# A gather-bound recommender kernel: the far weights moved behind the ids on one queue, and the last steps of TensorE put in another order with a second PSUM bank

## The chip, the cores and the metric

The kernel runs on one core of a Trainium2 chip. The metric is the device time of that core in microseconds, the median of repeated executions. All executions of this study were in the state called fast. They still fall into two kinds: on two occasions the kernel before took 13,197 to 13,298 us (medians), on three others 11,252 to 11,276 us, and within one occasion its runs were alike to 1.1%. Four of the five occasions are on record with a chip number, and the four chips differ; no chip was met twice, so whether the kind belongs to the chip or to the occasion is not shown. The two kinds are called **stall chips** and **quiet chips** below, and no total of one kind is compared with one of the other except to say how they differ.

## The reference

For each of 16,384 rows there are 69 ids of a user's history and one label id. Cut to what matters:

```python
u   = emb[batch_user]                      # (B, 69, 96)
ql  = emb[batch_label[:, 0]]               # (B, 96)
z   = concat([q, u, q - u, q * u])         # q is ql, repeated for the 69 fields
h   = dice(z @ W1 + b1, a1)                # 384 -> 64
att = (h @ W2 + b2) @ W3 + b3              # one number per field
pre = where(batch_user < ITEM_NUM, u * att, 0)
pooled = einsum('gf,bfe->bge', window, pre)           # 69 fields into 10 groups
h = dice(bn(concat([pooled, ql]) @ Wf1 + bf1), af1)   # 1056 -> 200
h = dice(bn(h @ Wf2 + bf2), af2)                      # 200 -> 80
return h @ Wf3 + bf3
# dice(x, a) = (a * (1 - p) + p) * x   with p = sigmoid(x), up to a constant near 1
```

## The kernel before

The rows are fetched by GpSimd (POOL), 128 at a time, with indirect DMAs: 8,832 gathers for the history and 128 for the labels. TensorE transposes each gathered tile, computes the hidden layer for a pair of chunks (8 gathers), turns it into attention rows, spreads these over partitions, and sums ("pools") the rows by group with the gathered tile as weights. There are 1,104 pairs in 32 blocks of 512 rows; after each block the top layers run.

The start. The ids of the first block and the near weights (those of the attention part) go on the queue of SyncE, the far weights (those of the top layers) on that of ScalarE. Nine small constants of the top layers' dice are made from the far weights on VectorE (DVE), in program order ahead of the first label columns:

```python
ids = {0: const.tile([P, NCOL], I32, name="ids0")}
nc.sync.dma_start(out=ids[0], in_=idx0)            # 140 KB
...
nc.sync.dma_start(out=wn, in_=near)                # 236 KB
wf = const.tile([P, FAR.width], F32, name="wf")
nc.scalar.dma_start(out=wf, in_=far)               # 1,209 KB
...
dice1 = [dice_weights(b, a, f"dice1_{i}") for i, (b, a) in enumerate(zip(bf1c, af1c))]
dice2 = dice_weights(bf2c, af2c, "dice2")
...
qs[0] = head_gather(0)         # 4 gathers of label rows
head_turn(0, qs.pop(0))        # 4 transposes, then DVE copies them to qT
head_rows(0)
```

The end. The last block's top layers run in four quarters of 128 rows, each in two halves (h = 0, 1) of 16 matrix products, written by the trace as 32 matmul records. A half is followed by its dice: two activations on ScalarE (ACT), then one DVE operation that reads the half's PSUM bank. All halves share the pool `ps_m`, which has one bank:

```python
ps_h = ctx.enter_context(tc.tile_pool(name="ps_h", bufs=2, space=PSUM))
ps_m = ctx.enter_context(tc.tile_pool(name="ps_m", bufs=1, space=PSUM))
...
def top1(n, cols, h, part, p1):
    if part == 0:
        p1 = ps_m.tile([DH, BLK], F32, tag="m", name=f"p1_{n}_{h}_{cols.start}")[:, cols]
    for k in range(part * KTOP // 4, (part + 1) * KTOP // 4):
        ...
        nc.tensor.matmul(p1, w[:, h * DH : (h + 1) * DH], x, start=(k == 0), stop=(k == KTOP - 1))
    if part < 3:
        return p1
    dice(x1s[n][:, h, cols], g1, p1, bf1c[h], dice1[h])
...
# quarter[r] is a list of steps: 0..3 first half, 4..7 second half, 8 layer 2, 9 layer 3
d = NPAIR
at(d, pool_of(c + 4), hidden_of(c + 7), pool_of(c + 5), *quarter[2][0:4], rows_of(c + 6, 2), *quarter[2][4:8])
at(d, quarter[2][8], spread_of(c + 6, 2), quarter[2][9], quarter[3][0])
at(d, pool_of(c + 6), pool_of(c + 7), lambda: store(B // P - 1), *quarter[3][1:])
```

In the trace TensorE's matmuls follow this order, and `quarter[2][4]` starts only after DVE has read the bank of `quarter[2][3]` (at 13139.47 us, after 0.39 us of waiting).

## Time and profile before

| Kernel before | |
|---|---|
| three runs | 13260.15, 13297.63, 13308.35 us |
| profiled execution | 13170.6 us |
| PE busy / POOL busy | 66% / 64% |
| from the rows of quarter 2 (L353) to the end | 13138.03 to 13170.6: 32.6 us |

The prediction shows the lines of the page and of both timelines. Two views that it does not show are worth having. The first is the list of what POOL waited for in this profile (columns: line, releaser, then total us, number of waits, longest wait in us):

```profile
POOL u L257 <- issue: 2367.4, 7751, 1.5
POOL u L257 <- remote: 978.9, 318, 7.4
POOL u L257 <- PE acc L397: 462.2, 107, 39.8
POOL u L257 <- PE ptr L313: 434.0, 201, 5.7
```

The first line is the 0.3 us between two gathers, thousands of times. The second, the largest of the rest, is of waits whose releaser the profile could not name. The last two are waits for TensorE: POOL had to stop until TensorE freed a buffer, once for 39.8 us. The second view is the busy time in the stretch from 20 to 160 us, in the columns named in the prediction:

```profile
20.00:160.00 140.00, 23.73 (x68) 8.52 (x68) 11.61 (x21) 10.74 (x16) 100.12 (x107) 0.59 0.18 38
```

TensorE has 68 matmul records in 140 us, while POOL makes 107 gathers at its usual pace and fills its buffers. TensorE stands still. For most of these stops the trace says only "issue", but for one it names a releaser, a copy on ScalarE that frees a PSUM bank:

```profile
168.25 1.09 PE L313 MATMUL ptr<-ident,u 128*96 128x128 f32 x4 [26.09 <-ACT uT L325]
```

So TensorE does not stand alone: ScalarE and DVE stand too. The first sigmoid of the hidden layer (L344) starts at 68.90 us, 31.1 us after the end (37.81) of the last matmul record that it needs, and ScalarE was idle for the last 19.8 of them. Over all 1,104 pairs ScalarE sat idle for 3.1 us on average between that end and the sigmoid; in f_after, a run on a quiet chip below, it is 0.05 us. By the trace, whose matmul ends are modelled, the stall lies between TensorE's results and the engines that read them.

### The profile page before, as it was taken

How to read it: one execution, taken by the hardware profiler on the slowest of the kernel's cores; microseconds unless marked ns; L12 is line 12 of the kernel's file. 1: busy time of each engine (PE TensorE's matmuls, PEld its weight loads, DVE VectorE, ACT ScalarE, POOL GpSimd, SP SyncE). 2: the span in 40 equal slices, each digit the busy share in tenths (PEclk: the TensorE clock that was granted, in tenths of full speed). 3: DMA queues.
4: the chain of work that ended last, by engine and by line, in shares of the span. 5: the costliest groups of instructions: out<-in, count | busy, mean ns of one | idle time of the engine just before them, and what ended most of it. 6: DMA issues, size and time to landing. Idle time of an engine off the chain costs nothing.

```text
span 13170.6 us, 108463 instructions
## 1 busy us (share of the span) xinstructions
PE 8747.3 (66%) x41797; PEld 4554.2 (35%) x41797; DVE 3029.0 (23%) x5325; ACT 3167.1 (24%) x4969; POOL 8455.0 (64%) x8966
## 2 busy tenths in 40 slices
PE   3666666667666676666766667666666666676667
PEld 2333333333333333333333333333333333333334
DVE  2222222222222222222222222222222222222222
ACT  1222222222222222222222222222222222222222
POOL 6666666666666666666666666666666666666664
PEclk6777777777777777767777777777777777777777
DMA  1111111111111111111111111111111111111111
GB/s 40 35 35 34 34 34 37 34 36 34 34 36 34 35 35 35 37 34 34 35 34 37 33 35 34 34 36 35 35 35 33 36 34 35 35 35 35 35 34 22
DMA packets 288946, 454.19 MB, mean 34 GB/s; under 512 B 143538, under 2 KB 143922, under 8 KB 288306
## 3 DMA queue, kind: packets, MB, share of 16 engines
q0 software_dynamic: 286720, 440.98, 16.0%
q8 instruction: 335, 5.49, 0.2%
q1 hardware_dynamic: 1570, 5.04, 0.1%
q14 instruction: 177, 1.45, 0.0%
q10 hardware_dynamic: 144, 1.24, 0.0%
HBM read 446.61 MB, written 0.07 MB: 34 GB/s over the span
## 4 chain that ended last, share of the span: by engine, by line
PE 54%; issue 20%; another core or an unknown queue 16%; POOL 4%; ACT 3%; DVE 3%; DMA 1%; DVEq 0%; POOLq 0%
PE acc L397 11%; PE ptr L313 9%; PE ph L338 9%; PE ph L342 8%; PE p L436 7%; PE prow L353 4%; POOL u L257 3%; PE patt L370 1%; DVE quT L316 1%; PE pa L362 1%; ACT uT L325 1%; ACT y L345 1%; PE ph L335 1%; PE pc L290 1%
## 5 line engine op out<-in xcount | busy, mean ns | idle before, releaser
L257 POOL DMA_INDIRECT u<-in_rows,ids x8832 | 8333.2, 944 | 4552.4 <-issue 2367.4
L397 PE MATMUL acc<-rw,u 128*96 128x20 f32 x16384 | 1922.1, 260 | 1844.3 <-issue 1436.2
L397 PEld LDWEIGHTS acc<-rw,u 128*96 128x96 f32 x16384 | 1911.1, 197 | 2083.9 <-issue 1613.1
L313 PE MATMUL ptr<-ident,u 128*96 128x128 f32 x8832 | 1594.5, 316 | 1395.4 <-issue 1099.1
L325 ACT COPY uT<-ptr 96x512 f32<-96x512 f32 x2208 | 1283.3, 581 | 3091.3 <-DVE quT L316 1905.9
L313 PEld LDWEIGHTS ptr<-ident,u 128*96 128x96 f32 x8832 | 1079.1, 143 | 2732.2 <-issue 2182.7
L344 ACT ACTIVATE y<-ph 128x512 f32<-128x512 f32 x1104 | 659.3, 597 | 5104.0 <-remote 2661.7
L342 PE MATMUL ph<-quT,wn 96*64 96x512 f32 x4416 | 1693.6, 744 | 165.9 <-issue 158.6
L346 DVE TENSOR_TENSOR y<-ph,y 128x512 f32<-128x512 f32 x1104 | 763.5, 692 | 4287.1 <-ACT y L345 2399.0
L338 PE MATMUL ph<-uT,A 128*64 128x512 f32 x4096 | 1631.8, 800 | 145.8 <-issue 142.8
L316 DVE TENSOR_TENSOR quT<-ptr,qT 96x512 f32<-96x512 f32 x2048 | 1337.6, 680 | 1419.3 <-remote 892.2
L406 DVE COPY pooled<-acc 96x160 f32<-96x160 f32 x1008 | 429.6, 426 | 3547.6 <-remote 2121.3
L345 ACT ACTIVATE y<-y,wn,na1c 128x512 f32<-128x512 f32 x1104 | 897.8, 813 | 36.7
L342 PEld LDWEIGHTS ph<-quT,wn 96*64 96x64 f32 x4416 | 449.0, 172 | 1201.8 <-issue 1199.3
L353 PE MATMUL prow<-y,v 128*32 128x512 f32 x2208 | 629.5, 787 | 254.1 <-issue 150.2
L436 PE MATMUL p<-pooled,wf 96*100 96x512 f32 (+1 forms) x1400 | 616.5, 583 | 0.0
L338 PEld LDWEIGHTS ph<-uT,A 128*64 128x64 f32 x4096 | 280.6, 162 | 683.7 <-issue 664.9
L355 ACT COPY row<-prow 128x512 f32<-128x512 f32 (+1 forms) x277 | 161.8, 584 | 1421.8 <-remote 878.8
L370 PE MATMUL patt<-ident,row 128*128 128x128 f32 x1108 | 241.2, 338 | 277.6 <-issue 203.7
L436 PE MATMUL p<-pre,V 96*100 96x512 f32 (+1 forms) x700 | 372.7, 665 | 40.6 <-issue 25.8
L436 PEld LDWEIGHTS p<-pooled,wf 96*100 96x100 f32 x1400 | 233.7, 179 | 291.7 <-issue 291.6
L375 DVE SCALAR_TENSOR_TENSOR rw<-patt,bb,wn 128x320 f32<-128x320 f32 x554 | 273.4, 534 | 142.2 <-remote 64.3
(66 smaller groups left out, 2139.8 us busy)
## 6 DMA issues: line engine op xcount, KB each, us to landing
u<-in_rows,ids POOLq DMA_INDIRECT x8832
ids<-in_idx SPq DMA_DIRECT2D x8, 560.0 KB
q<-in_emb,ids POOLq DMA_INDIRECT x128
wf<-in_far ACTq DMA_DIRECT2D x1, 1209.0 KB
wn<-in_near SPq DMA_DIRECT2D x1, 236.0 KB
ids<-in_idx SPq DMA_DIRECT2D x1, 140.0 KB
out<-r SPq DMA_DIRECT2D x1, 63.5 KB
out<-r SPq DMA_DIRECT2D x1, 0.5 KB
```

The costliest lines, as they stand in the source:

```text
L257: nc.gpsimd.indirect_dma_start(out=dst, out_offset=None, in_=table, in_offset=bass.IndirectOffsetOnAxis(ap=index, axis=0),)
L313: nc.tensor.transpose(ptr[:, t * P : (t + 1) * P], u[:, 4 * j + t, :], ident)
L316: nc.vector.tensor_tensor(quT[:, j, :].rearrange("e (s f) -> e s f", f=FM), ptr.rearrange("e (s f) -> e s f", f=FM), by_field(q[:, k * NS ...
L325: nc.scalar.copy(uT[j][0:E], ptr)
L338: nc.tensor.matmul(p, As[n % 2][:, k // 4, :], uT[j], start=True, stop=False)
L342: nc.tensor.matmul(p, Wp, quT[:, j, :], start=False, stop=True)
L344: nc.scalar.activation(y, ph, AF.Sigmoid, scale=S_DICE)
L345: nc.scalar.activation(y, y, AF.Identity, bias=a1c, scale=na1c)
L346: nc.vector.tensor_mul(y, ph, y)
L353: nc.tensor.matmul(pr[32 * k : 32 * (k + 1), :], v2, ys[b + k], start=True, stop=True)
L397: nc.tensor.matmul(pa[:, j, 2 * t : 2 * t + 2, :].rearrange("e n g -> e (n g)"), u[:, 4 * j + t, :], rw[:, t, j, :], start=True, stop=True,)
L436: nc.tensor.matmul(p1, w[:, h * DH : (h + 1) * DH], x, start=(k == 0), stop=(k == KTOP - 1))
```

## The change

The intent at the start is to let the first gather go sooner: ids first, then near weights, then the 1,209 KB that nobody wants yet, all on one queue. The intent at the end is to fill TensorE's waits for dice with independent work (the attention rows' spread and the last two pools), and to let a second half start while the first half's bank is still being read. The instructions are the same in kind and number; they only move.

```diff
-    nc.scalar.dma_start(out=wf, in_=far)
+    nc.sync.dma_start(out=wf, in_=far)
...
         if part == 0:
-            p1 = ps_m.tile([DH, BLK], F32, tag="m", name=f"p1_{n}_{h}_{cols.start}")[:, cols]
+            banks, tag = (ps_h, "h") if n == NBLK - 1 and cols.start >= BLK // 2 and h == 1 else (ps_m, "m")
+            p1 = banks.tile([DH, BLK], F32, tag=tag, name=f"p1_{n}_{h}_{cols.start}")[:, cols]
...
-    at(d, pool_of(c + 4), hidden_of(c + 7), pool_of(c + 5), *quarter[2][0:4], rows_of(c + 6, 2), *quarter[2][4:8])
-    at(d, quarter[2][8], spread_of(c + 6, 2), quarter[2][9], quarter[3][0])
-    at(d, pool_of(c + 6), pool_of(c + 7), lambda: store(B // P - 1), *quarter[3][1:])
+    at(d, pool_of(c + 4), hidden_of(c + 7), pool_of(c + 5), *quarter[2][0:4], rows_of(c + 6, 2), quarter[2][4])
+    at(d, spread_of(c + 6, 2), *quarter[2][5:8], pool_of(c + 6), quarter[2][8], pool_of(c + 7))
+    at(d, quarter[2][9], quarter[3][0], lambda: store(B // P - 1), *quarter[3][1:])
```

## The prediction

> **What bounds the kernel now.** I read the page first (busy shares, slices, costliest groups), then the busy time by stretch, then the timelines of the first 70 us and the last 40 us, then the chain of work that ended last, in order of time, over the same last 40 us.
>
> The page says that no engine is full:
>
> ```profile
> PE 8747.3 (66%) x41797; PEld 4554.2 (35%) x41797; DVE 3029.0 (23%) x5325; ACT 3167.1 (24%) x4969; POOL 8455.0 (64%) x8966
> L257 POOL DMA_INDIRECT u<-in_rows,ids x8832 | 8333.2, 944 | 4552.4 <-issue 2367.4
> ```
>
> A gather costs 0.94 us on POOL and 0.30 us until the next, 1.25 us in all; 8960 gathers (8832 rows, 128 labels) at 1.25 us are 11,200 us, well under the span of 13,170.6 us. So POOL waits some 1,970 us for buffers that TensorE frees. TensorE sets the pace: 1,104 pairs of chunks in 13,170 us are 11.9 us a pair against 10.0 us of gathers, and its clock is at 0.73 on average, with stalls that the trace calls only "issue" (at the start, two pairs take 44.8 us, for example from 81.45 to 126.25 us). The change touches none of this steady part. It touches the first 10 us and the last 38 us, so this is a prediction of about ten microseconds in 13,300.
>
> The start, from the timeline of the first 70 us:
>
> ```profile
> 0.74 0.40 ACTq L155 DMA_DIRECT2D wf<-in_far  x1
> 0.75 0.40 SPq L142 DMA_DIRECT2D ids<-in_idx  x1
> 1.21 0.44 SPq L153 DMA_DIRECT2D wn<-in_near  x1
> ...
> 7.04 1.10 POOL L257 DMA_INDIRECT q<-in_emb,ids  x1 [5.73 <-DMA ids<-in_idx]
> 7.26 0.22 DVE L163 TENSOR_TENSOR Cq<-wn 96x64 f32<-96x64 f32 x1 [5.18 <-DMA wn<-in_near]
> ```
>
> POOL can gather nothing before the first ids (140 KB) are there, and waits 5.73 us for them; the 1,209 KB of far weights, wanted by nobody then, go beside them from the other queue. The trace's DMA packet records, read by queue, show it: far weights from 2.0 to 6.4 us, ids from 3.0 to 6.5 us with some engines' last one at 6.42 us, near weights from 5.9 to 7.1 us.
>
> The end, from the timeline of the last 40 us. Columns: start, duration, engine, line; in brackets the idle time just before and what ended it.
>
> ```profile
> 13135.75 2.35 PE L436 MATMUL p<-pooled,wf 96*100 96x128 f32 x20
> 13138.03 1.05 PE L353 MATMUL prow<-y,v 128*32 128x512 f32 x4
> ...
> 13139.47 1.34 PE L436 MATMUL p<-pre,V 96*100 96x128 f32 x10 [0.39 <-DVE x L421]
> ...
> 13144.58 0.67 PE L447 MATMUL p<-x,wf 100*80 100x128 f32 x4 [1.37 <-DVE x L421]
> ...
> 13146.60 0.38 PE L455 MATMUL p<-wf,x 80*128 80x1 f32 x2 [0.97 <-DVE x L421]
> ...
> 13147.32 1.46 PE L436 MATMUL p<-pre,V 96*100 96x128 f32 x8 [0.33 <-DVE res L456]
> 13148.57 2.64 PE L397 MATMUL acc<-rw,u 128*96 128x20 f32 x16
> 13151.73 2.75 PE L397 MATMUL acc<-rw,u 128*96 128x20 f32 x16 [0.52 <-DVE pooled L406]
> ...
> 13160.54 1.33 PE L436 MATMUL p<-pre,V 96*100 96x128 f32 x10 [1.37 <-DVE x L421]
> ```
>
> All gathers are done by then (the last is issued at 13051.5 us), and TensorE's own order is the path: every wait shown is one for the dice step of a top half or for an eviction, and the two pools that could fill them stand behind them in the order. The busy time by stretch (columns PE, PEld, DVE, ACT, POOL, then clock) adds the second cost:
>
> ```profile
> 13139.50:13144.60 5.10, 3.73 (x33) 3.52 (x33) 0.35 (x1) 1.09 (x3) 0.00 (x0) 1.00 0.00 0
> 13144.60:13148.60 4.00, 2.70 (x19) 2.32 (x20) 1.06 (x4) 0.85 (x2) 0.00 (x0) 0.92 0.00 0
> 13148.60:13154.50 5.90, 5.38 (x34) 5.27 (x34) 0.42 (x1) 0.00 (x0) 0.00 (x0) 0.50 0.01 3
> 13154.50:13160.50 6.00, 4.67 (x25) 4.46 (x25) 1.03 (x3) 0.86 (x2) 0.00 (x0) 0.69 0.04 11
> ```
>
> After the gappy stretch around 13144 us the clock is halved: sixteen pool matmuls take 2.45 to 2.75 us there and 1.46 us at full clock (13128.05 us).
>
> **What the Trainium skill says.** "DMA: Bandwidth & Descriptors", section "Queues, rings and completion order": each DMA engine goes round the queues that have work, packet by packet, and takes one queue's descriptors in order. The packet records above agree: two queues interleaved from 3.0 us on; on one queue the ids should pass first. "TensorE: Matmul & The Clock Gate", section "Part 1: The HAM clock gate": an idle window of about 3.4 us sends the array to half clock. The stretch at 0.50 agrees in kind, though TensorE was busy for 2.70 of the 4.00 us before it. "Perfetto Trace Analysis", section "Optimizing Tensor Performance": independent matmul groups should rotate through different PSUM banks so that an eviction overlaps the next group. That is what the second halves' own bank does; before, the first matmul of a second half waits for the DVE that reads the first half (13139.47 and 13160.54 us).
>
> **The change, part by part.**
>
> Start. Far weights now go behind ids and near weights. The first packet of the queue that was served first came 2.01 - 0.74 = 1.3 us after its issue, so ids packets could start at 2.0 us (at 3.0 us if that queue is simply slower). They are 128 packets of 55 ns over 16 engines, 8 x 55 ns = 0.45 us, so the last ends at 2.5 to 3.4 us instead of 6.46. From there to the gather took 7.04 - 6.46 = 0.6 us. First gather at 3.1 to 4.0 us: **3.0 to 3.9 us earlier**. Near weights follow in 8 x 78 ns = 0.6 us, so the set-up on DVE moves as much. Far weights: 8 packets an engine at 429 ns are 3.4 us, done near 7.5 us; their first reader in DVE's order is the nine dice constants (10.45 us before), ahead of the copy of qT (14.03 us before, about 10.6 us after). No wait expected. I count 3 us, as the stalls of the first 170 us may swallow a little.
>
> End. I walk TensorE's new order at full clock from the end of the first half of quarter 2, at 13138.1 us = 0. A top matmul costs 3.75 us / 32 = 0.117 us. Rows (1.0) to 1.0; first 8 matmuls of the second half, in the other bank without a wait (0.94), to 1.9; spread (0.46) to 2.4 (its row copy is ready at 1.64); 24 more (2.8) to 5.2; pool (1.46) to 6.65 in place of the dice wait of 1.3; layer 2 (0.66) to 7.3; pool (1.46) to 8.8 in place of the next dice wait (eviction of the former pool ends at 7.1); layer 3 (0.3) to 9.1; a wait until 9.45 for DVE, which now evicts the pool (0.42) before it reads layer 3 (0.20); 8 matmuls to 10.4; the store's transpose (0.3) to 10.7; 24 to 13.5; second half of quarter 3, no wait, 3.75 to 17.25. From there to the end nothing changes: 13170.6 - 13164.3 = 6.3. Sum 23.6 us, against 13170.6 - 13138.1 = 32.5 before. **End 8.9 us shorter.** Of these, about 5 us are waits (0.4 + 1.4 + 1.0 + 0.5 + 1.4, and the DVE wait of 0.3 stays) and 4 us are the half clock (1.0 + 1.3 of the pools, 0.5 of the eight, some 1.3 of the 24). As no TensorE wait above 0.5 us is left before the last dice, the half clock should not come; if it does, 5 us remain. I take 8.
>
> Sum: 3 + 8 = 11 us, 13297.6 - 11 = **13287 us**. No instruction is added or removed; work only moves.
>
> **The rivals.** (1) The ids gain does not reach the end: TensorE paces the kernel and stalls for 20 us at a time in the first 170 us, POOL fills all its buffers by about 152 us and then waits. For it: POOL is ahead anyway. Against: TensorE's own first transposes wait for gathers of that moment (1.0 to 1.2 us idle each, "DMA u"), so its whole start moves. Then 8 us are left: 13290 us. (2) The half clock stays in the tail, as its windows may fall otherwise: end 4 to 5 us shorter, 13290 to 13292 us. (3) Far weights or something behind them become a wait at the start: they land beyond 11 us and hold DVE in front of qT; loses 1 to 2 us of the 3. (4) Noise rules: the three runs before span 48 us, and the profiled execution took 13172 us, 1% less. TensorE's stalls, not the work, make that spread, and a shift of 3 us at the start can deal them anew. This is the largest term by far for the time that will be read.
>
> **Range and chances.** The mechanism gives 13285 to 13293 us; the spread of runs gives about 25 us either way for a median of three, with a longer tail downwards because of the profiled execution. Range 13225 to 13330 us. A step of 2% is 266 us, more than twice the gap between the fastest execution seen and the median: 0.02 faster, 0.97 within 2%, 0.01 slower.
>
> **What would show it right or wrong.** In the changed profile: first gather at 3 to 4 us, not 7.04, with the idle time before it near 2 us; near weights' first reader at about 4 us; nine dice constants without an idle time ahead of them. In the tail: no DVE x wait before the first matmul of a second half; two pools at about 1.5 us each; clock 1.00 from the last pool to the last second half; about 24 us from the end of quarter 2's first half to the end of the span. It would be wrong if ids still land after 5 us, if a second half waits for its bank, if the clock is again 0.50 after the pools, or if the whole time moves by more than 100 us, which the changed parts cannot explain.

## The result, and the profile after

| Same chip, six runs each | before | after |
|---|---|---|
| median, us | 13289.36 | 13282.84 |
| range, us | 13260.15 to 13308.35 | 13243.29 to 13305.56 |
| ratio after/before | | 0.9994, 95% interval 0.9975 to 1.0012 |

Ratios are the mean time of one kernel's fast runs over that of the other's of the same rounds, so not quite the ratio of the medians quoted. The verdict is "same"; the interval is about 24 us either way and cannot show a gain of 11. The two profiled spans (13170.6 before, 13284.2 after) must not be subtracted: they differ by 114 us because of stalls far from the changed parts. What can be compared is the changed parts themselves.

The start, from the timeline of the profile after (columns as in the prediction):

```profile
1.68 0.42 SPq L155 DMA_DIRECT2D wf<-in_far  x1
...
3.23 1.10 POOL L257 DMA_INDIRECT q<-in_emb,ids  x1 [1.92 <-DMA ids<-in_idx]
3.92 0.22 DVE L163 TENSOR_TENSOR Cq<-wn 96x64 f32<-96x64 f32 x1 [1.85 <-DMA wn<-in_near]
...
9.53 0.15 DVE L222 TENSOR_SCALAR dice<-wf 100x1 f32<-100x1 f32 x1 [2.35 <-DMA wf<-in_far]
...
9.85 0.42 PE L281 MATMUL pq<-ident,q 128*96 128x128 f32 x1 [3.26 <-DMA q<-in_emb,ids]
...
12.70 0.69 DVE L282 COPY qT<-pq 96x512 f32<-96x512 f32 x1 [2.53 <-PE pq L281]
```

The first gather is at 3.23 us instead of 7.04, and the near weights' first reader at 3.92 instead of 7.26. But DVE now waits 2.35 us for the far weights, and the copy to qT is at 12.70 us, only 1.3 us before the 14.03 of the kernel before. The trace's DMA packet records, on the zero of the timeline, suggest why. On the one queue the ids pass first, from 1.77 to 2.61 us; the far weights' packets run from 3.06 to 8.94 us, and the first packet of a gathered label row comes at 7.38 us, 4.2 us after the gather started. Before, that was 9.06 - 7.04 = 2.0 us, and the far weights were out of the way by 6.17 us. So the label rows seem to wait in the DMA engines beside the far weights; `f_held` below tests it.

The end, from the timeline of TensorE in the profile after (the two added lines make L436 into L438, L447 into L449):

```profile
13259.66 1.05 PE L353 MATMUL prow<-y,v 128*32 128x512 f32 x4
13260.64 1.12 PE L438 MATMUL p<-pre,V 96*100 96x128 f32 x8
...
13264.78 1.46 PE L397 MATMUL acc<-rw,u 128*96 128x20 f32 x16
13266.08 0.68 PE L449 MATMUL p<-x,wf 100*80 100x128 f32 x4
13266.76 1.53 PE L397 MATMUL acc<-rw,u 128*96 128x20 f32 x16
...
13268.84 1.14 PE L438 MATMUL p<-pre,V 96*100 96x128 f32 x8 [0.34 <-DVE res L458]
...
13270.85 3.51 PE L438 MATMUL p<-pooled,wf 96*100 96x128 f32 x20
13274.20 1.25 PE L438 MATMUL p<-pre,V 96*100 96x128 f32 x10
```

Neither second half (13260.64 and 13274.20) has an idle time ahead of it. The two pools take 1.46 and 1.53 us instead of 2.64 and 2.75, with layer 2 between them. The one wait left in this stretch is 0.34 us. From the rows (L353) to the end of the span it is 13284.2 - 13259.66 = 24.5 us, against 32.6: 8.1 us shorter. The twenty matmuls at 13270.85 take 3.51 us, though, where the same group takes 2.35 at full clock. The busy time by stretch, same profile:

```profile
13261.10:13266.20 5.10, 5.10 (x52) 4.89 (x51) 0.97 (x3) 1.12 (x3) 0.00 (x0) 1.00 0.00 0
13266.20:13270.20 4.00, 3.66 (x33) 3.31 (x33) 1.29 (x5) 0.86 (x2) 0.00 (x0) 0.95 0.01 4
13270.20:13274.20 4.00, 4.00 (x26) 4.00 (x25) 0.29 (x1) 0.00 (x0) 0.00 (x0) 0.62 0.05 14
13274.20:13277.90 3.70, 3.70 (x36) 3.64 (x34) 0.35 (x1) 0.87 (x3) 0.00 (x0) 1.00 0.01 2
```

TensorE was busy in 3.66 of the 4.00 us from 13266.2, and still its mean clock in the next 4 us was 0.62. In the trace's clock records the granted clock is only ever 1.00 or 0.50, in pieces of 3.41 us or multiples of it (but for the last piece): before, it is 0.50 from 13147.94 us for 10.24 us, after, from 13269.81 us for 3.41 us. The lowered clock has shrunk, not gone.

So the local intervals moved as intended: 3.8 us at the first gather, 8.1 us in the tail. What is open is whether both arrive in the total, and which part of the change does what.

### The profile page after: what moved, and what is told of

Same layout as the page of the kernel before. It is cut to its first block, busy times and chain, and to the rows that moved or that the text cites. A ratio compares the mean times of both kernels' runs of the same rounds, so it can differ in the third digit from the quotient of the medians.

```text
span 13284.2 us, 108461 instructions
## 1 busy us (share of the span) xinstructions
PE 8859.7 (67%) x41797; PEld 4576.5 (34%) x41797; DVE 3037.9 (23%) x5325; ACT 3167.4 (24%) x4969; POOL 8476.9 (64%) x8966
## 4 chain that ended last, share of the span: by engine, by line
PE 54%; issue 21%; another core or an unknown queue 14%; POOL 5%; DVE 3%; ACT 2%; DMA 1%; DVEq 0%; POOLq 0%
PE acc L397 11%; PE ptr L313 9%; PE ph L338 9%; PE ph L342 9%; PE p L438 7%; POOL u L257 5%; PE prow L353 4%; PE patt L370 1%; DVE quT L316 1%; PE pa L362 1%; ACT uT L325 1%; PE ph L335 1%; PE pc L290 1%; ACT y L345 1%
## 5 line engine op out<-in xcount | busy, mean ns | idle before, releaser
L313 PE MATMUL ptr<-ident,u 128*96 128x128 f32 x8832 | 1637.3, 319 | 1651.3 <-issue 1300.8
L342 PE MATMUL ph<-quT,wn 96*64 96x512 f32 x4416 | 1722.9, 749 | 211.3 <-issue 200.3
L353 PE MATMUL prow<-y,v 128*32 128x512 f32 x2208 | 669.4, 785 | 285.0 <-issue 187.8
L438 PE MATMUL p<-pooled,wf 96*100 96x512 f32 (+1 forms) x1400 | 621.5, 587 | 2.4 <-issue 2.4
L438 PE MATMUL p<-pre,V 96*100 96x512 f32 (+1 forms) x700 | 368.8, 664 | 23.1 <-issue 13.1
L438 PEld LDWEIGHTS p<-pooled,wf 96*100 96x100 f32 x1400 | 236.4, 181 | 295.0 <-issue 294.8
```

What stands on the lines that cost most here:

```text
L313: nc.tensor.transpose(ptr[:, t * P : (t + 1) * P], u[:, 4 * j + t, :], ident)
L342: nc.tensor.matmul(p, Wp, quT[:, j, :], start=False, stop=True)
L353: nc.tensor.matmul(pr[32 * k : 32 * (k + 1), :], v2, ys[b + k], start=True, stop=True)
```

## The experiments

Theory: both gains reach the end and add up. Rival: TensorE paces the kernel, so an earlier first gather is swallowed, and only the end counts. A further rival is that the far weights, now in the way of the label rows, cost what the ids gained.

### A short version, to get the noise out (s_before, s_after, s_start, s_end)

Each is cut to two blocks (69 pairs, 1,024 rows). They are **wrong on purpose**: the other rows of the output are never written, so the relative error is nan. `s_start` has the far weights' queue alone, `s_end` the new order and the second bank alone.

```diff
-NPAIR = NBLK * NCH // 2
+NRUN = 2
+NPAIR = NRUN * NCH // 2
+FIRST = (NPAIR - 8) % 4      # lines up the groups of four pairs at the end
...
-        if n == NBLK - 1 and k >= EARLY:
+        if n == NRUN - 1 and k >= EARLY:
```

> The kernel before, cut to its first two blocks of rows (69 pairs of chunks instead of 1,104; the other 15,360 results are not written, so it is wrong on purpose), so that its start and its end are the same instructions but the steady part, whose stalls make the spread of 50 us, is one sixteenth as long. All theories: about 69 pairs at 11.9 us and some 80 us of slow first pairs, an estimate of 850 to 950 us, with a spread of runs of a few us instead of 50. Start and tail as in the full kernel: first gather near 7.0 us, copy of qT near 14.0 us, 32 to 33 us from the end of quarter 2's first half to the end of the span.

> The changed kernel cut in the same way. Theory A (both parts reach the end): 9 to 11 us less than the cut kernel before, about 1%: some 8 us from the tail, 1 to 3 us from the start. Theory B (only the tail reaches the end, the start is swallowed by TensorE's stalls in the first 170 us): 7 to 9 us less. Theory C (the stalls are dealt anew by any shift, and the changes are lost in it): less than 4 us apart, or an order of the runs that does not repeat.

> Cut kernel with the start part of the change alone (far weights on the ids' queue, behind ids and near weights). The profile of the full changed kernel has the first gather at 3.23 us, 3.8 us earlier, but the copy of qT only 1.3 us earlier (12.70 against 14.03 us). Theory S1 (gathers set the start): 3 to 4 us less than the cut kernel before. Theory S2 (the first gathers' rows wait behind the far weights on the DMA engines): about 1.3 us less in the start, and 0 to 2 us less in all. Theory S3 (the stalls swallow it): 0 us, within 1 us.

> Cut kernel with the end part of the change alone (new order and the second halves' own bank). Theory A and B: 7 to 9 us less than the cut kernel before, the tail 24 to 25 us long instead of 32 to 33, and within 2 us of the whole change. Rival (half clock stays in the tail): tail 27 to 29 us, 4 to 5 us less in all.

| four runs each | median, us | minus s_before | last gather starts | rows of quarter 2 to the end |
|---|---|---|---|---|
| s_before | 771.20 | | 707.1 | 32.3 |
| s_start | 764.10 | -7.1 | 703.5 | 32.4 |
| s_end | 763.33 | -7.9 | 707.7 | 24.4 |
| s_after | 752.98 | -18.2 | 703.3 | 25.8 |

The absolute time missed my expectation: 771 us, because this chip had no long stalls. The kernel before at full size took 11252.48 us on it (7 runs). The signs are clear, the sizes are not: s_before alone spreads from 762.39 to 772.70 us, and by means instead of medians the differences are -5.3, -6.7 and -16.0. What the profiles add is more exact: the start part moves the last gather by 3.6 us and leaves the tail alone, the end part does the opposite. The list of POOL's waits in s_before explains why the start reaches the end here:

```profile
POOL u L259 <- issue: 159.4, 523, 0.3
```

The gaps between gathers are of 0.3 us; the only longer wait of POOL is the 5.2 us for the first ids. On this chip the gathers are the bound, not TensorE.

### The parts at full size on a quiet chip (f_after, f_start, f_end, f_order)

All give correct results. `f_after` is the change itself; the others are the kernel before with one part: `f_start` the queue line, `f_end` the order and the bank, `f_order` the order alone, with all halves left in `ps_m`.

```diff
 f_start:
-    nc.scalar.dma_start(out=wf, in_=far)
+    nc.sync.dma_start(out=wf, in_=far)
 f_order:
-    at(d, pool_of(c + 4), ..., *quarter[2][4:8])      # the three old lines
+    at(d, pool_of(c + 4), ..., quarter[2][4])         # the three new ones
 f_end: the lines of f_order, and
+            banks, tag = (ps_h, "h") if n == NBLK - 1 and cols.start >= BLK // 2 and h == 1 else (ps_m, "m")
```

> The whole change at full size, again, in case it meets a chip without TensorE's long stalls, such as the one of the cut kernels, where the kernel before took 11,252 us and repeated to about 5 us. There POOL never waits for a buffer, so gathers at 1.25 us set the pace and both ends of the kernel add in full. Theory Q (gathers bound on such a chip): 3.8 us from the start and 7 to 8.5 us from the tail, 11 to 12.5 us less than before (0.10 to 0.11%). Theory R (the cut kernels' 18 us hold at full size): 15 to 20 us less. On a chip with the stalls: within 0.3% of before, sign unclear.

> Start part alone at full size. Gathers bound: 3.5 to 4 us less than before, equal to the earlier first gather (7.04 to 3.23 us), although the first label rows reach TensorE only 1.3 to 2.4 us earlier. Rows behind the far weights bind instead: about 1.3 us less. On a chip with the stalls: unclear.

> End part alone at full size. Gathers bound: the last gather is issued at the same time as before, and the tail from the end of quarter 2's first half to the end is 24 to 25.5 us instead of 32.3: 7 to 8.5 us less. On a chip with the stalls the tail is the same in the profile, the total unclear.

> New order of the end alone, at full size, without the bank of its own: first and second halves share one bank as before. By the walk through TensorE's order both halves' dice waits of 1.4 us come back (in quarter 2 rows fill 1.0 us of it, so 0.4 us), the rest of the gain stays: tail 25 to 27 us, 5.5 to 7 us less than before. Rival (the bank is what matters and the order alone only moves waits): less than 3 us.

The chip was quiet: the kernel before 11254.23 us (65 runs, 11250.55 to 11260.55).

| | median, us (runs) | minus before | ratio, 95% interval | rows of quarter 2 to the end |
|---|---|---|---|---|
| f_after | 11240.27 (21) | -14.0 | 0.9987, 0.9980 to 0.9994 | 24.3 |
| f_start | 11250.12 (13) | -4.1 | 0.9995, 0.9987 to 1.0004 | 32.6 |
| f_end | 11244.77 (21) | -9.5 | 0.9990, 0.9984 to 0.9997 | 24.6 |
| f_order | 11247.95 (21) | -6.3 | 0.9993, 0.9986 to 0.9999 | 27.1 |

**The parts add up**: 4.1 + 9.5 = 13.6 against 14.0 (by means 5.0 + 10.2 = 15.2 against 14.7). f_after falls between its two theories, and f_end's 9.5 us is above the 7 to 8.5 expected. The interval of f_start alone still includes no change, so the profile is asked as well. All gathers of f_start, then of f_end (columns: count, shortest/median/longest in ns, start of the first and of the last in us):

```profile
L257 POOL DMA_INDIRECT u<-in_rows,ids x8832: 940/944/1096, 8.4 to 11189.3; - x197
```

```profile
L257 POOL DMA_INDIRECT u<-in_rows,ids x8832: 940/944/1092, 12.4 to 11192.5; - x197
```

With the far weights behind the ids the first row gather is 4.0 us earlier and the 8,832nd still 3.2 us earlier. So most of it arrives. f_after agrees with its last gather at 11189.0, f_order (without the queue line) with 11192.7. These 3.2 us and the 8.0 us of f_end's tail make 11.2, less than the 14.0 of the totals. The profiles show where such a difference can come from: the stretch from the last gather to the rows of quarter 2, which no edit touches, took 21.3 us in f_after, 27.9 in f_start, 31.4 in f_end and 31.5 in f_order, at mean clocks of 1.00, 0.87, 0.84 and 0.84. Single profiles of different kernels can therefore not be subtracted here either; the medians of 13 to 65 runs average this out in part. In f_after POOL's waits begin with

```profile
POOL u L257 <- issue: 2532.8, 8311, 0.3
...
```

and all others too, but for the 1.9 us for the first ids, have a longest of 0.3 us. Compare a steady millisecond of f_after, and then of the kernel before on the stall chip (POOL's busy column is the fifth, `755.89 (x802)`; the 0.76 and 0.74 behind it are TensorE's clock):

```profile
5000.00:6000.00 1000.00, 802.46 (x3764) 410.81 (x3762) 274.42 (x469) 285.31 (x445) 755.89 (x802) 0.76 0.20 41
```

```profile
5000.00:6000.00 1000.00, 698.84 (x3250) 357.85 (x3251) 234.65 (x408) 243.94 (x383) 649.89 (x690) 0.74 0.17 35
```

802 gathers in 1,000 us are 1.247 us each, which is what a gather and its gap take (0.944 + 0.30): POOL never stops. On the stall chip there are 690, and TensorE does less in the same time at nearly the same mean clock. The stretch from 20 to 160 us of f_after stands against the 68 matmul records of the kernel before on the stall chip:

```profile
20.00:160.00 140.00, 96.58 (x359) 42.23 (x359) 50.26 (x100) 37.07 (x57) 106.04 (x112) 0.63 0.20 40
```

There are 359, at a clock of 0.63 against 0.59: the stall is not a slow clock.

The tail part of the change is about the same on both kinds of chip. The start part is in full view only where gathers are the bound.

In f_order the two waits that the shared bank causes are there still:

```profile
11225.67 1.12 PE L436 MATMUL p<-pre,V 96*100 96x128 f32 x8 [0.39 <-DVE x L421]
...
11240.95 1.34 PE L436 MATMUL p<-pre,V 96*100 96x128 f32 x10 [1.37 <-DVE x L421]
```

Their sum, 1.76 us, is most of the 2.5 us between the tails of f_order (27.1) and f_end (24.6). By total time the bank on top of the order is worth 11247.95 - 11244.77 = 3.2 us (by means 2.3, each mean with a standard error of 0.8 to 0.9).

How much harm do the far weights do by the time it matters? The first matmuls of the hidden layer, in f_after and then in f_end:

```profile
31.03 1.98 PE L338 MATMUL ph<-uT,A 128*64 128x512 f32 x4
```

```profile
34.48 1.98 PE L338 MATMUL ph<-uT,A 128*64 128x512 f32 x4
```

The lead is 3.45 us, though the copy to qT started only 2.3 us earlier (11.85 against 14.19). The matmul needs the eight gathers of its pair, and these follow POOL's clock, not that of qT.

### The bank alone, and two repairs of the start (f_bank, f_held, f_small)

`f_bank` is the kernel before with the second bank and the old order. `f_held` is the change with the far weights issued only after the first pair, and their readers moved back. `f_small` is the change with the first ids split, so that the 2 KB of label ids travel ahead of the rest.

```diff
 f_bank (to the kernel before):
+            banks, tag = (ps_h, "h") if n == NBLK - 1 and cols.start >= BLK // 2 and h == 1 else (ps_m, "m")
 f_held (to the change):
-    nc.sync.dma_start(out=wf, in_=far)
...
+    def far_load():
+        nc.vector.memset(wf[0:1, 0:1], 0.0)
+        nc.sync.dma_start(out=wf, in_=far)
...
+    at(1, far_load)
+    at(3, far_prep)                 # the nine dice constants
-        at(2 + 2 * f, lambda f=f: tail_weights(f))
+        at(4 + 2 * f, lambda f=f: tail_weights(f))
 f_small (to the change):
-    nc.sync.dma_start(out=ids[0], in_=idx0)
+    lab0 = const.tile([P, NQ], I32, name="lab0")
+    nc.sync.dma_start(out=lab0, in_=idx0[:, NT:NCOL])
+    nc.sync.dma_start(out=ids[0][:, 0:NT], in_=idx0[:, 0:NT])
...                                 # the first label gathers read lab0
```

> The bank of its own for the second halves alone, in the old order, at full size. By the walk it removes the 0.4 us wait in quarter 2 and the 1.4 us wait in quarter 3: tail (from quarter 2's rows to the end) 30.8 us instead of 32.6, 1.8 us less in all; the half clock of the pools stays, since the dice waits before layers 2 and 3 stay. Rival (bank and order are independent, each worth what it adds to the other): 3.2 us less, the difference between the medians of the whole end part and of the order alone.

> The whole change, but the far weights are loaded only after DVE's work on the first pair (a one-element write to their tile by DVE holds the transfer back), and their readers come later. In the changed kernel the first label rows waited behind the far weights on the DMA engines: first gather 3.25 us, its rows at TensorE 9.1 to 9.9 us. Held back, rows should land some 2.3 us after their gather as before the change, TensorE's first transpose of labels near 6 us and the copy of qT near 10.5 us instead of 12.3. Theory G (the pace of gathers is the path, TensorE catches up with it within the first pair): the total is within 2 us of the whole change. Rival (the rows that waited are on the path): 1.5 to 2.5 us less than the whole change.

> The whole change, with the first ids split: the four label columns in a transfer of their own (2 KB), the rest behind it. If the path at the start is issue, landing, first gather: the first gather starts at 2.5 to 2.8 us instead of 3.25, all gathers follow, 0.5 to 0.7 us less than the whole change, too small to be sure of in the total but plain in the profile. Rival (the 280 columns cost nothing, it is the landing that takes the time, or the fifth gather now waits for the second transfer): first gather unchanged, or idle time before the first row gather.

This chip had the stalls: the kernel before 13197.48 us (51 runs, 13163.47 to 13255.01).

| | median, us (runs) | ratio, 95% interval | rows of quarter 2 to the end |
|---|---|---|---|
| f_bank | 13199.03 (22) | 0.9998, 0.9989 to 1.0006 | 30.3 |
| f_held | 13197.11 (14) | 0.9993, 0.9980 to 1.0005 | 24.3 |
| f_small | 13188.95 (22) | 0.9991, 0.9983 to 0.9999 | 24.2 |

No total here decides anything about ten microseconds: the standard deviation of one run is 19 us, against 2.7 us on the quiet chip. f_small, which contains the whole change, is 11 us below the kernel before by means (13188.2 against 13199.3), of the size of the quiet chip's gain, at the edge of its interval. f_held contains it as well and is 5.7 us below by means. The local intervals decide more.

*f_bank.* The tail shortens by 2.3 us, from 32.6 to 30.3, between the 1.8 of the walk and the 3.2 of the rival. The pools stay where they were, and slow:

```profile
13147.96 2.64 PE L397 MATMUL acc<-rw,u 128*96 128x20 f32 x16
13151.11 2.75 PE L397 MATMUL acc<-rw,u 128*96 128x20 f32 x16 [0.51 <-DVE pooled L406]
```

These are the durations of the kernel before, and of f_start, which has the old order on a quiet chip. So the lowered clock at the pools does not come from the waits at the bank. At the pools it goes when the order changes (1.46 and 1.48 us in f_order, where the bank's waits remain); further on, f_order still has one piece of 3.41 us at half clock, from 11234.41 us.

*f_held.* The far weights' packets ran from 32.87 to 36.83 us, out of the way. The first label packet came at 5.04 us, 1.8 us after the first gather at 3.24, and the copy to qT started at

```profile
10.64 0.69 DVE L288 COPY qT<-pq 96x512 f32<-96x512 f32 x1 [3.51 <-PE pq L287]
```

That is 2.1 us earlier than in the profile after, and it is the 10.6 us that the prediction had worked out without the far weights' traffic. **The traffic is the cause** of the later head (the label rows' way to qT). The edit holds back the far weights and, behind them on the queue, the next blocks' ids (two loads of 560 KB). The far weights are the likelier part: in the profile before, packets of the next ids ran from 6.23 to 9.57 us, and the label rows still came after 2.0 us. The first hidden matmul was at 31.08 us. In the profile after it comes only at 70.39, behind a stall, so the run to compare with is f_after (31.03, on a quiet chip): the gain seems gone within the first pair.

*f_small.* The first gather was at 2.92 us instead of 3.23; I had expected 0.5 to 0.7 us from it and got 0.3. The bytes of the ids are a small part of what the first gather waits for.

### Both repairs on a quiet chip (f_both)

`f_both` is the change with f_held's and f_small's edits together. It tells whether the pace of the gathers is all there is (then only f_small's few tenths of a microsecond come on top of the change), or whether an earlier head is worth its 2 us as well.

> The whole change with both additions to its start: far weights held back, and the label columns of the first ids in a transfer of their own. First gather near 2.9 us as in the run with the split ids, the labels' rows some 2.3 us after their gathers as in the run with the far weights held back, copy of qT near 10.3 us. On a chip without the long stalls (before 11,250 to 11,260 us): theory G (pace of gathers is the path) 14 to 15 us less than before, as the whole change with 0.3 us more; rival (late label rows are on the path) 16 to 17 us less. On a chip with the stalls (before near 13,200 or 13,290 us): 5 to 20 us less, which tells nothing between the two.

The chip was quiet: the kernel before 11276.48 us (25 runs), f_both 11261.18 us (21 runs), ratio 0.9987, 0.9980 to 0.9994. That is 15.3 us by medians and 14.8 by means, against 14.0 and 14.7 for the change on another quiet chip. From its timeline:

```profile
2.75 1.10 POOL L265 DMA_INDIRECT q<-in_emb,lab  x1 [1.44 <-DMA lab<-in_idx]
...
9.79 0.69 DVE L290 COPY qT<-pq 96x512 f32<-96x512 f32 x1 [2.21 <-PE pq L289]
```

The head is 2 us earlier than in f_after (11.85 us) and the first gather 0.5 us, but the first hidden matmul (30.14 us) only 0.9 us earlier than in f_after and 0.3 us than in f_start, and the total follows the gather. The margin to the rival is about 1 us across two chips, so this is support rather than proof. As a version to use, f_both has no gain over the change that these runs can show.

## Why the prediction was right, and where it was not

**The size and the verdict.** 13287 us was predicted, 13282.84 measured, within 2% as expected. On its own that proves little, since the runs' spread hides the change, and that the two are so close is partly luck: the 13297.6 from which the 11 us were taken became 13289.4 with three more runs. The quiet chip gives it: 14.0 us against the 11 counted, of which the start 4.1 against 3 and the end 9.5 against 8. Both sizes had been cut back for doubts. The uncut ones (3.0 to 3.9, and 8.9) are nearer.

**First gather at 3.1 to 4.0 us.** Right: 3.23 us, with small errors that nearly cancel. All packet times of the prediction are 0.25 us late against the timeline (far weights from 1.76 to 6.17 us, ids from 2.72 to 6.22, near weights from 5.63 to 6.82). So from issue to first packet it was 1.0 us and not 1.3, while in the profile after the ids' packets took 0.84 us (1.77 to 2.61) and not 0.45; from the last packet to the gather it was 0.6 us, as counted.

**"TensorE sets the pace."** True of the profile it was read from, where POOL waits in stretches of up to 39.8 us. Not true of the kernel: on three quiet chips the gathers are the bound and no wait of POOL after that for the first ids exceeds 0.3 us in the profiles read. The 44.8 us from 81.45 to 126.25 are one pair (8 transposes and 8 hidden matmul records), not two. Rival 1, that the ids' gain does not reach the end, is refuted there by the last gather (3.2 us earlier in f_start than in f_end). On stall chips it stays undecided, as rival 4, noise, said it might.

**Far weights done near 7.5 us, no wait.** The reader was at 9.53 us after a wait of 2.35, so this failed in the profile after; in f_after the same reader was at 7.70 us after 0.58. The step that failed was the transfer's rate: eight packets an engine at 429 ns, back to back, as if the engines were theirs alone. The packet records of the profile after show the next ids' packets among them from 6.48 us and the label rows' from 7.38; how much of the delay is due to these, and why f_after was spared, is not separated. It also overlooked the opposite effect, that the label rows come later: 4.2 us from gather to first packet instead of 2.0. So rival 3 happened, and cost the head 1 to 2 us as it said (qT at 12.70 us in the profile after and 11.85 in f_after, instead of 10.6). It did not cost the total, because the head is not the path: f_end and f_after still differ by 3.45 us at the first hidden matmul.

**The tail.** Predicted 23.6 us from the end of the first half of quarter 2, measured 24.5 (the first half ends at 13259.73). The order of TensorE's steps, the fillers and the DVE wait of 0.3 us (0.34) were as walked. The term that was off is the clock: the twenty matmuls took 3.51 us instead of 2.35, and 1.16 us is a little more than the whole gap of 0.9. "As no TensorE wait above 0.5 us is left before the last dice, the half clock should not come" was wrong; the clock sank to 0.62 after a stretch that was 92% busy (3.66 of 4.00 us). Rival 2 happened in a small way. As an estimate from the clock's pieces, (10.24 - 3.41) / 2 = 3.4 of the 8.1 us gained are clock and 4.7 are waits, where the prediction counted 4 and 5.

**Order or bank.** The prediction split the gain by waits and clock, not by edit. By edit, on the quiet chip: the order 6.3 us, the bank 3.2 more.

**What stays open.** Why some chips have the long stalls and others none. The traces place the stall between TensorE's results and their readers (3.1 us of idle ScalarE a pair, against 0.05), the mean clock differs by only 0.02 (0.73 and 0.75), and no experiment here tells causes apart. Nor is it known why the clock sank in the last stretch.

## What to carry to other kernels

Put the bytes that the first waiter needs at the front of a queue, and then look at what the bulk behind them delays; it matters only if what it delays is on the path. On an engine that works in order, fill waits for an eviction with independent work first, and give consecutive accumulation groups different banks for the waits that are left. Judge a gain of ten microseconds in ten thousand by local intervals of the traces and on a chip where the spread allows it, and check on more than one chip which engine is the bound.

## What the Trainium skill lacked or had wrong

- "TensorE: Matmul & The Clock Gate", section "Part 1: The HAM clock gate", has the array go to half clock after an idle window of about 3.4 us. In the profile after, no idle time of TensorE between 13255.0 and 13274.2 us was longer than 0.34 us, and the clock was at 0.50 from 13269.81 us for 3.41 us. The part also lets frequent short idle times between groups lower the clock, but how little is enough is not stated.
- "DMA: Bandwidth & Descriptors", section "Specifications", gives about 0.6 us of first-byte latency for transfers from the sync and scalar queues. In the profile after, the first ids packet came at 1.77 us: 1.0 us after the start of the issuing instruction (0.75), 0.6 us after its end (1.16). The page does not say from which it counts; from the end it agrees. The gather that waited for all 140 KB started at 3.23 us.
- No page that I read says that a large load in flight delays the rows of indirect gathers issued meanwhile: 4.2 us from the gather's start to its first packet with 1,209 KB of weights in flight, 1.8 us with them held back (and the next ids behind them).
- No page that I read says that the same program can have a different bound on another chip or occasion: 13,197 to 13,298 us with TensorE standing still for up to 29.6 us at a time (51.8 to 81.45 us in the profile before), 11,252 to 11,276 us without, at a mean clock of 0.73 and 0.75.
